# A decoder layer whose cross-attention keeps its SyncE transfers in program order, with the output steps of a batch one unit later

## The chip, the core and the metric

The kernel runs on one core of a Trainium2 chip. The core has a matrix engine (TensorE, "PE" in the profile, with its weight loads as "PEld"), three engines for elementwise work (VectorE "DVE", ScalarE "ACT", GpSimd "POOL") and SyncE ("SP"), which in this kernel issues most of the transfers. All transfers run on 16 DMA engines that the issuing engines share. The metric is the time of one execution on the device in microseconds; less is better.

## What is computed

One decoder layer in float32 over 16 batches of 128 tokens and 1024 channels. With `ln` for the layer norm:

```python
x = x + self_attn(ln(x))
x = x + cross_attn(ln(x), ctx, ctx)
x = x + ffn(ln(x))            # 4-bit weights, silu(gate) * up, down
```

The change touches only the cross-attention, which for each batch computes (8 heads of 64, the 128 tokens are the channels of its 1x1 convolutions, the 1024 model channels are its positions):

```python
qh = softmax(Wq @ q, over the 64 of a head) * 64**-0.5
kh = softmax(Wk @ k, over the positions)
context = kh @ vh.T                       # per head, 64 x 64
out = Wo @ (context.T @ qh) + bo
out = out / max(norm(out, over channels), 1e-12) * g * sqrt(128)
```

## The kernel before, in words

The program has three stages. In the first, self-attention runs and the first five blocks of the gate and up weights are unpacked beside it. The second is the cross-attention of batches 8 to 15 and then 0 to 7; in the profile it runs from about 250 us to about 850 us, the last part overlapping the third. The third is the feed-forward network, by nested matrix products with fewer multiplications, to the end.

**Units and ticks.** The cross-attention is cut into units, and after each unit `tick()` runs what is due. `later(n, fn)` puts `fn` off until the n-th tick from then; what falls due in one tick runs in the order in which it was put off. A batch has eight units, alternating: a key unit for the batch after it (`key_unit`, matmuls `kq<-wk_sb,cx`, then the exponential `ek` on ACT, and two ticks later the context matmuls `kx<-ek,cxt`) and a query unit for itself (`query_unit`, matmuls `kq<-wq_sb,xn`, then `qe` on ACT). The four query units of a batch are called `oc` 0 to 3.

**The way of a query unit.** `weigh` divides by the softmax sums: DVE reduces `qden`, POOL multiplies `qe` (132 us for all 64). `turn` then transposes 32 x 32 squares on DVE (`kt<-qe`) and stores the result to a buffer in DRAM (`kd<-kt`, line 817). One tick later `load` reads it back in another arrangement in four transfers (`qs<-kd`, line 822). `qs` has five buffers, each batch fills four. A later step consumes them: `project_out` has four `piece` steps of TensorE (`mm<-qs,m_sb`), one for each `qs`, then `norms` (`mm<-sq,ones`), then on DVE, one tick apart, a scaling of `y`, an addition to the residual `X`, the statistics of the next layer norm, its shift, and `turned`, which stores `X` to DRAM through POOL's queue and puts the normalised rows through a transpose (`kt<-xn`) and four more SP transfers (`xt<-kt`, line 579).

**When the outputs run.** The tuple `when` gives the ticks for the four pieces and `norms`, counted from the start of the batch, so a 12 is the fourth unit of the following batch:

```python
if len(ahead) == 2:
    when = (12, 13, 14, 15, 16, 1, 1)
elif ahead:
    when = (12, 13, 14, 15, 16, 1, 0)
else:
    when = (10, 10, 11, 11, 12, 1, 0)
```

**What sets the order of instructions.** A scheduler orders the instructions of every engine when the kernel is built. `InOrder` wraps an engine, so that each instruction given through it keeps its place in program order among the others given so. In this stage TensorE and VectorE are wrapped (`tensor`, `vector`; the profile shows their instructions under line 63). ScalarE, GpSimd and SyncE are not, so the scheduler may place a transfer of SyncE ahead of or behind others of the same queue. SyncE carries out its queue in order: a transfer that waits holds back all behind it.

**What lies around it.** At the start of the stage SP loads the weights of the cross-attention (`wk_sb`, `wq_sb`, the two halves of `wvo`, `xbo_sb`, `gs_sb`), the context of two batches in both arrangements (`cx`, `cxt`), and in `wo_again` the output weights of the self-attention, for the last four batches of which `give_half` still has to run (matmuls `mm<-wo_again,oT`, from the first tick on). At the end, SP loads the first weights of the feed-forward network (`w`, line 1081; the first pair through POOL's queue), and its matmuls (`p<-b,w`, line 1156) take the place of units, with a tick after each.

Of the kernel before, what the change touches and what calls it, by code (L numbers as in the profile page):

```python
# [18 lines left out]
P = 128  # L19
# [47 lines left out]
def decoder_layer(  # L67
# [28 lines left out]
    nc = tc.nc  # L96
# [435 lines left out]
    first.close()  # L532

    tensor, vector = InOrder(tc, nc.tensor), InOrder(tc, nc.vector)

# [33 lines left out]
    def turn_rows(b, xn, pool):  # L571

        kt = pool.tile([P, 4, 2 * JC, Q], F32, name="kt")
        vector.transpose(
            kt.rearrange("p c m t -> p m c t"), xn.rearrange("p m (c i) -> p m c i", c=4)
        )
        xt = xt_all[PASSES.index(b - b % HB)][b % HB]
        for a in range(4):
            nc.sync.dma_start(
                xt[a].rearrange("c i n j t -> i c (n j t)"),  # L580
                kt[ts(a, Q)].rearrange("i c m t -> i c (m t)"),
            )
# [36 lines left out]
    def later(n, fn):  # L619
        pend.append([n, fn])  # L620

    def tick():
        for p in pend:
            p[0] -= 1
        due = [p for p in pend if p[0] <= 0]
        for p in due:
            pend.remove(p)
        for p in due:
            p[1]()

    if True:
        wq_sb = bw.tile([P, HIDDEN], F32, name="wq_sb")
        wk_sb = bw.tile([P, HIDDEN], F32, name="wk_sb")
        wvo = b0.tile([P, 2, 4, S], F32, name="wvo", tag="xn2")
        wv_sb, xwo_sb = wvo[:, 0], wvo[:, 1]
        g_sb = bs.tile([P, HEADS, S], F32, name="g_sb")
        xbo_sb = bs.tile([P, 1], F32, name="xbo_sb")
        gs_sb = bs.tile([P, 1], F32, name="gs_sb")
        ones = bs.tile([P, P], F32, name="ones")
        nc.sync.dma_start(wk_sb, xwk)  # L640
        nc.sync.dma_start(wq_sb, xwq)
        nc.sync.dma_start(wv_sb, xwv.rearrange("(r p) s -> p r s", p=P))
        nc.sync.dma_start(xwo_sb, xwo.rearrange("(r p) o -> p r o", p=P))
        nc.sync.dma_start(xbo_sb, xbo)
        nc.sync.dma_start(gs_sb, xg)
        vector.tensor_scalar(gs_sb, gs_sb, math.sqrt(S), None, ALU.mult)
        vector.memset(ones, 1.0)
        if plain:
# [5 lines left out]
        def note(*both):  # L654
            if plain:
                for t, v in zip(totals, both):
                    t = t[:, : v.shape[1]]
                    nc.gpsimd.tensor_tensor(t, t, v, ALU.add)
# [14 lines left out]
        def mix_weights():  # L673

            D = DIM_HEAD
            for e in range(2):
                ps = bps.tile([P, 4, S], F32, name="mm")
                for r in range(4):
                    tensor.matmul(
                        ps[:, r, :],  # L680
                        wv_sb[ts(e, D), r, :],
                        xwo_sb[ts(e, D), r, :],
                        start=True,
                        stop=True,
                    )
                dst = g_sb.rearrange("p (r e) o -> p e r o", e=2)[:, e]
                nc.scalar.mul(dst, ps, D**-0.5)

        def load_ctx(b):
            c = bcx.tile([P, C], F32, name="cx")  # L690
            nc.sync.dma_start(c, cx[b])
            ct = bct.tile([P, NB, S], F32, name="cxt")
            nc.sync.dma_start(ct, cxt[b])
            return c, ct

        def key_shift(c_sb):
# [86 lines left out]
        def query_unit(xn, pair, qs, wait):  # L783

            wide = [P, 2 * HEADS, DIM_HEAD]
            ps = bpk.tile([P, 2, 512], F32, name="kq")
            for i in range(2):
                tensor.matmul(
                    ps[:, i, :], xn[:, ts(2 * pair + i, P)], wq_sb, start=True, stop=True
                )  # L790
            heads = ps.rearrange("p i (h d) -> p (i h) d", d=DIM_HEAD)
            qe = b3.tile(wide, F32, name="qe")
            if plain:
                nc.scalar.activation(qe, heads, AF.Exp)  # L794
            else:
                mx = small.tile([P, 2 * HEADS], F32, name="qmx")
                vector.tensor_reduce(mx, heads, AX.X, ALU.max)
                vector.tensor_tensor(qe, heads, mx.unsqueeze(2).to_broadcast(wide), ALU.subtract)
                nc.scalar.activation(qe, qe, AF.Exp)

            def weigh():
                den, rec = (small.tile([P, 2 * HEADS], F32, name=n) for n in ("qden", "qrec"))
                vector.tensor_reduce(den, qe, AX.X, ALU.add)
                vector.reciprocal(rec, den)
                nc.gpsimd.tensor_tensor(qe, qe, rec.unsqueeze(2).to_broadcast(wide), ALU.mult)  # L805
                note(den, rec)

            def turn():  # L810
                kt = bkt.tile([P, 4, NB, Q], F32, name="kt")
                vector.transpose(
                    kt.rearrange("p c n j -> p n c j"),
                    qe.rearrange("p h d -> p (h d)").rearrange("p (n c j) -> p n c j", c=4, j=Q),
                )
                kd = dram.tile([4, Q, 4, NB, Q], F32, name="kd", tag="kd", bufs=3)
                nc.sync.dma_start(kd.rearrange("a i c n j -> (a i) c n j"), kt)

                def load():
                    qt = qs[pair] = bqs.tile([P, 4, NB, Q], F32, name="qs", tag="qs")  # L820
                    for c in range(4):
                        nc.sync.dma_start(  # L822
                            qt[ts(c, Q)], kd[:, :, c].rearrange("a i n j -> i a n j")
                        )

                later(1, load)

            later(2, weigh)
            later(wait, turn)

        def turned(b):
# [65 lines left out]
        def rows(b):  # L897
            xn = b0.tile([P, C], F32, name="xn2", tag="xn2")
            row_shift(b, vector)
            normalise_act(xn, X[b], b)  # L900
            return xn
# [3 lines left out]
        def operand(q):  # L905

            b12 = blocks[0, 1]
            if q == 7:
                T0[7] = b12
                vector.tensor_tensor(b12, blocks[1, 1], b12, ALU.subtract)  # L910
                return
            t = T0[q] = xres.tile(
                [P, TOKENS, JC, Q], F32, name=f"T{q}", tag={5: "X0", 6: "X2", 4: "X4"}[q]
            )
            a, b = {
                5: (b12, blocks[0, 0]),
                6: (blocks[1, 1], T0.get(5)),
                4: (blocks[1, 0], T0.get(6)),
            }[q]
            vector.tensor_tensor(t, a, b, ALU.subtract)  # L920


        batches = [p + i for p in PASSES for i in range(HB)]
        ctxs = {b: load_ctx(b) for b in batches[:2]}
        wo_again = []
        for d in range(2):
            wo_again.append(bqs.tile([P, C], F32, name="wo_again", tag="qs"))
            nc.sync.dma_start(wo_again[d], wo[ts(d, P)])
        mix_weights()
        xns = {batches[0]: rows(batches[0])}  # L930

# [9 lines left out]
        for k, b in enumerate(batches):  # L941
            ahead = batches[k + 1 : k + 3]
            qs = {}


            if len(ahead) == 2:
                when = (12, 13, 14, 15, 16, 1, 1)
            elif ahead:
                when = (12, 13, 14, 15, 16, 1, 0)
            else:  # L950
                when = (10, 10, 11, 11, 12, 1, 0)
            project_out(b, qs, keys[b], when)
            if ahead:
                later(5, lambda n=ahead[0]: xns.update({n: rows(n)}))
            if len(ahead) == 2:
                later(2, lambda n=ahead[1]: ctxs.update({n: load_ctx(n)}))

            for n, q in {B - 3: [(5, 5)], B - 2: [(3, 7), (7, 6)], B - 1: [(6, 4)]}.get(k, ()):
                later(n, lambda q=q: operand(q))
            for oc in range(4):  # L960
                if ahead:
                    key_unit(ctxs[ahead[0]], oc, keys[ahead[0]])
                    tick()
                query_unit(xns[b], oc, qs, 4 if len(ahead) == 2 else 3)
                tick()
# [59 lines left out]
    with ExitStack() as gs:  # L1025

        def pool(name, bufs, **kw):
            return gs.enter_context(tc.tile_pool(name=name, bufs=bufs, reuse_waits="tile", **kw))

        cw = pool("c_w", 5)  # L1030
        ct = pool("c_t", 4)
# [868 lines left out]
```

## Time and profile before

| | |
|---|---|
| time, median of 3 runs | 2260.39 us (2260.33 to 2260.86) |
| time of the profiled execution | 2262.39 us |
| its span, first to last instruction | 2260.5 us |
| mean granted TensorE clock | 0.996 |
| TensorE matmuls busy | 2207.0 us, 98% of the span |
| VectorE busy | 1517.2 us, 67% |
| GpSimd busy | 555.6 us, 25% |
| ScalarE busy | 472.0 us, 21% |
| SP's transfers | 377.72 MB, 53.5% of the 16 DMA engines' time |

All times inside the execution are microseconds from the start of the span. "Busy" of TensorE counts pipelined matmuls. A wait is the idle time of an engine ahead of an instruction, with what ended it; a float32 matmul appears as two instructions, so four matmuls of a piece are "x8". "SPq" is SP's queue, and an entry there is the issue of a transfer, not its duration.

### The profile page before, as it was taken

What the parts mean: (1) busy time and instruction counts of PE and PEld (TensorE: products, weight loads), DVE (VectorE), ACT (ScalarE), POOL (GpSimd) and SP (SyncE); (2) the same over time, 40 slices, a digit from 0 to 9 for tenths busy, and PEclk for the clock granted to TensorE, in tenths of its full rate; (3) what the DMA queues carried; (4) which work ended last, traced back from release to release, by engine and by line L of the source; (5) the groups of instructions that cost most, each with busy time, mean ns of one, the idle gap of its engine ahead of it and who ended that gap; (6) DMA issues with size and microseconds to landing.
All of it is one profiled execution on the core that took longest, in us unless ns stands there. A gap on an engine that the chain in (4) does not pass through costs nothing.

```text
span 2260.5 us, 24112 instructions
## 1 busy us (share of the span) xinstructions
PE 2207.0 (98%) x8330; PEld 1517.4 (67%) x8330; DVE 1517.2 (67%) x2055; ACT 472.0 (21%) x651; POOL 555.6 (25%) x543
## 2 busy tenths in 40 slices
PE   8999999999998999999999999999999999999998
PEld 7556555555555554444774478888888688888887
DVE  6997467767777738756787668787787546544462
ACT  2111234544454441111111111122121000000000
POOL 5452044344444410000330034444442000000000
PEclk9999999999999999999999999999999999999999
DMA  6435256676696478888739843554554974433731
GB/s 249 156 130 185 75 149 182 199 197 178 196 277 175 149 207 288 282 269 268 220 131 288 278 126 126 191 179 151 191 182 160 354 225 147 133 123 128 224 117 39
DMA packets 270835, 425.23 MB, mean 188 GB/s; under 512 B 28784, under 2 KB 130544, under 8 KB 270576
## 3 DMA queue, kind: packets, MB, share of 16 engines
q1 hardware_dynamic: 244624, 377.72, 53.5%
q0 software_dynamic: 8064, 27.27, 3.3%
q10 hardware_dynamic: 18016, 18.62, 2.6%
q8 instruction: 68, 1.11, 0.2%
q14 instruction: 63, 0.52, 0.1%
HBM read 265.62 MB, written 157.35 MB: 187 GB/s over the span
## 4 chain that ended last, share of the span: by engine, by line
PE 86%; DVE 6%; DMA 3%; issue 3%; SPq 1%; ACT 1%; POOL 1%; DVEq 0%; POOLq 0%; ACTq 0%
PE po L1779 21%; PE q L63 20%; PE p L63 18%; PE kq L63 8%; PE mm L63 6%; PE kx L63 4%; PE mm L396 4%; DMA qs<-kd 2%; PE mm L411 2%; PE p L1156 1%; DVE pa L63 1%; PE mm L292 1%; SPq L822 1%; DVE kt L63 1%; PE tr L343 1%
## 5 line engine op out<-in xcount | busy, mean ns | idle before, releaser
L63 PE MATMUL p<-b,w 128*128 128x512 f32 x560 | 246.4, 592 | 0.0
L63 PE MATMUL q<-ti,li 128*128 128x256 f32 x1008 | 233.7, 381 | 3.5 <-DVE ti L63 2.8
L63 POOL TENSOR_TENSOR li<-w 128x512 f32<-128x512 f32 x84 | 118.3, 1410 | 430.7 <-DMA w<-wu 241.1
L63 PEld LDWEIGHTS q<-ti,li 128*128 128x128 f32 x1008 | 192.1, 191 | 31.6 <-issue 2.8
L63 PEld LDWEIGHTS p<-b,w 128*128 128x128 f32 x560 | 106.4, 190 | 133.1 <-issue 129.4
L1779 PE MATMUL po<-wc,lc 128*128 128x256 f32 x840 | 183.4, 379 | 0.0
L63 PE MATMUL p<-T,w 128*128 128x512 f32 x400 | 177.2, 592 | 0.0
L1779 PEld LDWEIGHTS po<-wc,lc 128*128 128x128 f32 x840 | 159.6, 190 | 21.7
L63 ACT COPY k<-q 128x512 f32<-128x512 f32 x126 | 73.7, 585 | 400.6 <-PE q L63 400.6
L63 PE MATMUL mm<-qs,m_sb 128*128 128x256 f32 x512 | 123.0, 384 | 21.2 <-DMA qs<-kd 21.2
L63 PEld LDWEIGHTS mm<-qs,m_sb 128*128 128x128 f32 x512 | 97.0, 191 | 64.7 <-issue 46.0
L63 PEld LDWEIGHTS p<-T,w 128*128 128x128 f32 x400 | 76.0, 190 | 95.7 <-issue 95.2
L805 POOL TENSOR_TENSOR qe<-qe,qrec 128x1024 f32<-128x1024 f32 x64 | 132.1, 2064 | 4.0 <-issue 0.2
L1779 PE MATMUL po<-wq,lq 128*128 128x256 f32 x560 | 126.7, 379 | 0.3 <-issue 0.3
L63 PE MATMUL kq<-wq_sb,xn 128*128 128x512 f32 x256 | 122.3, 602 | 0.0
L63 PE MATMUL kx<-ek,cxt 128*128 128x512 f32 x256 | 121.8, 598 | 0.0
L63 PE MATMUL kq<-wk_sb,cx 128*128 128x512 f32 x256 | 120.4, 592 | 0.0
L1779 PEld LDWEIGHTS po<-wq,lq 128*128 128x128 f32 x560 | 106.0, 190 | 15.9 <-issue 0.9
L63 DVE TENSOR_TENSOR pa<-pa,sz 128x1024 f32<-128x1024 int32 x86 | 113.8, 1324 | 2.5
L396 PE MATMUL mm<-xnT,wqkv_sb 128*128 128x512 f32 (+1 forms) x320 | 112.5, 507 | 0.0
L726 ACT ACTIVATE ek<-kq 128x1024 f32<-128x1024 f32 x64 | 65.5, 1023 | 182.1 <-PE kq L63 182.1
L63 DVE TENSOR_REDUCE qden<-qe 128x16 f32<-128x1024 f32 x64 | 76.4, 1194 | 29.6 <-ACT qe L794 29.6
(201 smaller groups left out, 3620.8 us busy)
## 6 DMA issues: line engine op xcount, KB each, us to landing
w<-wu SPq DMA_DIRECT2D x140, 256.0 KB, 3.6
lq<-h SPq DMA_DIRECT2D x140, 256.0 KB, 4.5
w<-wg SPq DMA_DIRECT2D x138, 256.0 KB, 2.8
kd<-kt SPq DMA_DIRECT2D x64, 512.0 KB, 3.0
qs<-kd SPq DMA_DIRECT2D x256, 128.0 KB, 4.1
h<-hc SPq DMA_DIRECT2D x80, 256.0 KB, 2.8
wq<-wd SPq DMA_DIRECT2D x70, 256.0 KB, 5.2
h<-h SPq DMA_DIRECT2D x60, 256.0 KB, 3.5
```

The lines of the kernel that those rows point to most:

```text
L63: return lambda *args, **kw: self._tc.keep_in_program_order(fn(*args, **kw))
L292: tensor.matmul(ps, oT[:, d, ts(b % BPT, S)], wo_d[d][:, ts(h, 512)], start=(d == 0), stop=(d == 1),)
L343: nc.tensor.transpose(tr[:, j, :], xn[:, ts(4 * h + j, P)], ident)
L396: nc.tensor.matmul(ps[:, tokens], wqkv_sb[:, f, c, :], xnT[:, c, tokens], start=(c == 0), stop=(c == CC - 1),)
L411: nc.tensor.matmul(ps, xnT[:, c, ts(i, S)], wqkv_sb[:, 4:6, c, :], start=(c == 0), stop=(c == CC - 1),)
L726: nc.scalar.activation(ek, ps, AF.Exp)
L805: nc.gpsimd.tensor_tensor(qe, qe, rec.unsqueeze(2).to_broadcast(wide), ALU.mult)
L822: nc.sync.dma_start(qt[ts(c, Q)], kd[:, :, c].rearrange("a i n j -> i a n j"))
L1156: tensor.matmul(ps, wt[:, j, :], T[q][:, :, j], start=(first == q and j == 0), stop=(q in (2, 3, 4) and j == JC - 1), skip_group_check=True,)
L1779: nc.tensor.matmul(bank[:, i, :], l[:, ts(i, S)], w,  start=(start and c == 0 and i % 2 == 0), stop=(stop and c == len(pairs) - 1), skip_g ...
```

## The change

A wrapper `sync = InOrder(tc, nc.sync)` is made beside those of TensorE and VectorE, and every transfer that the cross-attention issues on SyncE goes through it: the loads of weights and context at its start, `kd`, `qs`, `xt` and `wo_again`. The loads of the feed-forward network (`w`) and of the weight preparation stay outside. Besides, for a batch that has two more behind it, the four pieces and `norms` are due one tick later, and with `norms` all steps after it.

```diff
     tensor, vector = InOrder(tc, nc.tensor), InOrder(tc, nc.vector)
+    sync = InOrder(tc, nc.sync)
...
         for a in range(4):
-            nc.sync.dma_start(
+            sync.dma_start(
                 xt[a].rearrange("c i n j t -> i c (n j t)"),
...
-        nc.sync.dma_start(wk_sb, xwk)
-        nc.sync.dma_start(wq_sb, xwq)
-        nc.sync.dma_start(wv_sb, xwv.rearrange("(r p) s -> p r s", p=P))
-        nc.sync.dma_start(xwo_sb, xwo.rearrange("(r p) o -> p r o", p=P))
-        nc.sync.dma_start(xbo_sb, xbo)
-        nc.sync.dma_start(gs_sb, xg)
+        sync.dma_start(wk_sb, xwk)
+        sync.dma_start(wq_sb, xwq)
+        sync.dma_start(wv_sb, xwv.rearrange("(r p) s -> p r s", p=P))
+        sync.dma_start(xwo_sb, xwo.rearrange("(r p) o -> p r o", p=P))
+        sync.dma_start(xbo_sb, xbo)
+        sync.dma_start(gs_sb, xg)
...
             c = bcx.tile([P, C], F32, name="cx")
-            nc.sync.dma_start(c, cx[b])
+            sync.dma_start(c, cx[b])
             ct = bct.tile([P, NB, S], F32, name="cxt")
-            nc.sync.dma_start(ct, cxt[b])
+            sync.dma_start(ct, cxt[b])
...
                 kd = dram.tile([4, Q, 4, NB, Q], F32, name="kd", tag="kd", bufs=3)
-                nc.sync.dma_start(kd.rearrange("a i c n j -> (a i) c n j"), kt)
+                sync.dma_start(kd.rearrange("a i c n j -> (a i) c n j"), kt)
...
                     for c in range(4):
-                        nc.sync.dma_start(
+                        sync.dma_start(
                             qt[ts(c, Q)], kd[:, :, c].rearrange("a i n j -> i a n j")
                         )
...
             wo_again.append(bqs.tile([P, C], F32, name="wo_again", tag="qs"))
-            nc.sync.dma_start(wo_again[d], wo[ts(d, P)])
+            sync.dma_start(wo_again[d], wo[ts(d, P)])
...
             if len(ahead) == 2:
-                when = (12, 13, 14, 15, 16, 1, 1)
+                when = (13, 14, 15, 16, 17, 1, 1)
```

As built, the order of the instructions differs in these places. On SP, one batch in the steady part was `kd kd kd, qs qs, xt, qs, kd, cx, cxt, qs` (a `qs` stands for its four transfers) and is now `kd, qs, kd, qs, kd, xt, qs, kd, cx, cxt, qs`. At the start, SP's queue was `xbo_sb, gs_sb, cxt, cxt, wk_sb, wq_sb, wvo, wvo, cx, cx, wo_again, wo_again` and is now `wk_sb, wq_sb, wvo, wvo, xbo_sb, gs_sb, cx, cxt, cx, cxt, wo_again, wo_again`. On TensorE each piece and `norms` stand one unit later, so that `norms` now follows a key unit; the number of matmuls is the same. On VectorE `m_sb` now comes ahead of the scaling of `y`, and the statistics come after the next `qden`. At the end of the stage TensorE and SP have the same work in nearly the same order.

## The prediction

> **What bounds the kernel now.** I began with the page. TensorE is busy for 2207.0 of 2260.5 us and most of the chain that ended last is its work, so only TensorE's idle time and its clock can be gained. One group of the page has idle time in front of it on TensorE that this change can reach:
>
> ```profile
> PE 86%; DVE 6%; DMA 3%; issue 3%; SPq 1%; ACT 1%; POOL 1%; DVEq 0%; POOLq 0%; ACTq 0%
> L63 PE MATMUL mm<-qs,m_sb 128*128 128x256 f32 x512 | 123.0, 384 | 21.2 <-DMA qs<-kd 21.2
> ```
>
> Asked for the waits of TensorE from 293 to 765 us, the trace names nothing but these 21.2 us, in 10 waits: 1.5 to 2.1 us each and one of 4.3. So I laid one batch out in time: TensorE, SP's queue and the transposes of VectorE.
>
> ```profile
> 454.77 1.89 PE L63 MATMUL mm<-qs,m_sb 128*128 128x256 f32 x8
> 456.50 1.88 PE L63 MATMUL kx<-ek,cxt 128*128 128x512 f32 x4
> 458.22 1.88 PE L63 MATMUL kq<-wk_sb,cx 128*128 128x512 f32 x4
> 462.19 1.97 PE L63 MATMUL mm<-qs,m_sb 128*128 128x256 f32 x8 [2.10 <-DMA qs<-kd]
> ```
> ```profile
> 442.91 13.20 SPq L817 DMA_DIRECT2D kd<-kt  x3
> 456.20 4.12 SPq L822 DMA_DIRECT2D qs<-kd  x8
> 460.42 1.90 SPq L579 DMA_DIRECT2D xt<-kt  x4
> 462.57 2.03 SPq L822 DMA_DIRECT2D qs<-kd  x4
> ```
> ```profile
> 441.64 1.24 DVE L63 STREAM_TRANSPOSE kt<-qe 128x1024 f32<-128x1024 f32 x1
> 448.84 1.25 DVE L63 STREAM_TRANSPOSE kt<-qe 128x1024 f32<-128x1024 f32 x1
> 454.53 1.23 DVE L63 STREAM_TRANSPOSE kt<-qe 128x1024 f32<-128x1024 f32 x1
> ```
>
> The piece that waits is the fourth of the batch. By the ticks its operand (`oc` 3) is the transpose at 441.64, stored at 442.91. Its load, due a tick later, stands behind two further stores in SP's queue, and these wait for the transposes that end at 450.1 and 455.8. So it goes out at 456.2 instead of soon after 446, and TensorE, ready at 459.9 (458.22 and 1.72 of pace), starts at 462.19. The other pieces have over 10 us in hand. The list of SP's waits has this behind it: `kd` waits for the transpose 254.7 us in 48 times; a store early in the queue costs nothing, the load behind it does.
>
> **What the skill says.** The Trainium skill, DMA: Bandwidth & Descriptors, "Two DMAs through the same engine are not ordered", wants the issuing engine to wait for the first transfer's semaphore before a dependent one; the trace agrees (SP waits 14.7 us in all for `kd<-kt` ahead of `qs`), so every load costs SP the landing of its store. The same page, "Issuing engines are not separate DMA queues", has all transfers on the same 16 engines; at 248 to 256 us they are busy to 0.96 to 1.04, so added bytes there take time. TensorE: Matmul & The Clock Gate, "What's actually happening", puts the clock at half after an idle window of about 3.4 us; here also one wait of 2.1 us was followed by it, others of that length not. SBUF — State Buffer, "SBUF: two separate sides", has VectorE with two operands and GpSimd exclude each other; the trace agrees (a scaling of `y` takes 2.25 us beside GpSimd, 1.16 without).
>
> **The steady part.** What a batch costs without a wait: from the fourth piece at 331.26 to that at 395.61 lie two batches with one wait of 1.65 us, 64.35 us; from 428.60 to 462.19 one batch with one of 2.10, 33.59. The difference, 62.70 less 31.49, is 31.2 us without wait, and 0.25 us per wait beyond its idle time (restart). After two of the waits the clock is low:
>
> ```profile
> 596.00:600.00 4.00, 4.00 (x11) 2.55 (x12) 2.04 (x3) 1.26 (x2) 0.00 (x0) 0.64 1.04 279
> 600.00:604.00 4.00, 4.00 (x10) 1.85 (x9) 1.47 (x2) 2.43 (x4) 0.22 (x1) 0.93 0.81 279
> 729.00:733.00 4.00, 3.78 (x10) 2.78 (x11) 1.19 (x2) 1.01 (x2) 0.00 (x0) 0.66 1.06 275
> 785.00:789.00 4.00, 3.64 (x5) 1.68 (x6) 2.09 (x2) 1.44 (x2) 2.05 (x2) 0.59 1.02 273
> ```
>
> (The granted clock is the last but two.) That is 4 x 0.36 + 4 x 0.07 = 1.7 us each for the first two. In reach: 21.2 + 10 x 0.25 + 3.4 = 27.1 us.
>
> Does all of it go? In program order the load of `oc` 3 follows its own store: store at 442.9, landed about 3.0 us later (its row), four issues of 0.45: all out by 448, landed by 452. The piece is wanted at 459.9, and one unit later still (3.4 us). Each edit alone would cover the 2.25 us; I count 27.1 once. What is late next? SP: per batch 4 x (0.34 + 3.0 + 1.9) + 1.9 for `xt` + 0.7 for the contexts = 23.5 us of 31.2; behind a waiting load stands the next store, and behind that, with three `kt` buffers, a transpose. `qs` has five buffers: the load of the next batch's `oc` 1 is due at tick 16 and takes the buffer of the first piece, now at 13 instead of 12; three units are left. ScalarE: from `norms` to the mixing matmuls into its old PSUM bank there were two units (6.9 us) and is now one with the four small matmuls: about 4.3 us from the end of the first half, for an exponential (1.02) and a logarithm (0.6). VectorE: the shift now comes about 3 us later against TensorE; ScalarE's row normalisation (1.24) and the exponential (1.02) that the next `kx` needs queue behind it. Laying the durations end to end I find 1.1 to 2.5 us in hand there, the least anywhere. So nothing added: **-27.1**; if each of 13 batches lost 1 us there, -14.
>
> **The start.** The built order puts both `cxt` loads (2 x 512 KB), which went out at 221 us into idle DMA engines, behind `wk_sb`, which waits for the last self-attention matmul, and ahead of `wo_again`:
>
> ```profile
> 221.12 0.91 SPq L693 DMA_DIRECT2D cxt<-in_cxt  x2
> 245.80 0.33 SPq L640 DMA_DIRECT2D wk_sb<-in_xwk  x1
> 247.68 0.98 SPq L691 DMA_DIRECT2D cx<-in_cx  x2
> 248.76 0.84 SPq L928 DMA_DIRECT2D wo_again<-in_wo  x2
> ```
> ```profile
> 255.74 1.12 PE L63 MATMUL mm<-wo_again,oT 128*128 128x512 f32 x2 [0.19 <-DMA wo_again<-in_wo]
> 257.07 1.10 PE L63 MATMUL mm<-wo_again,oT 128*128 128x512 f32 x2 [0.21 <-DMA wo_again<-in_wo]
> ```
>
> TensorE already takes `wo_again` as it lands, so every added byte is on its path: 1.05 MB at the 369 to 393 GB/s of 252 to 256 us is 2.8 us, at the 291 GB/s of the whole burst (3.15 MB from 246.1 to 256.9) 3.6. I take **+2.8**, and for the clock after some 3 us of idle time **+1.5** (0 if it holds, 1.7 if not). The two more issues ahead (0.33 and 0.51) hide in this queue; `gs_sb` lands later, and VectorE meets it about where it does now (251.5). Bounds +2.8 and +5.3.
>
> **The end.** After 777.97 TensorE waits 5.5 us for the first `w`, which GpSimd issues at 782.28 behind a `qe` product that waits for VectorE, where `y`, a transpose and `X` precede `m_sb` and `qden`. Now `m_sb` and `qden` precede `y` and `X`, so the issue comes up to 3.3 us earlier; part is given back at the transpose chain that the first `p<-T,w` needs. I take **-1.5**, between -3.5 and +3 (the new order holds back a transfer). The feed-forward part has the same matmuls in the same order and goes to its end as before: 0, within 1.
>
> **The sum.** -27.1 + 2.8 + 1.5 - 1.5 = -24.3, on a span of 2260.5 us: 2236.2. The profiled execution took 2262.39, 1.9 more than its span and 2.0 more than the median of the runs, so the median should be 2260.4 - 24.3 = **2236 us**.
>
> **Rivals.** (a) The forecast, with the ends of its terms from -28.8 (start +2.8 and no clock loss, end -3.5, feed-forward -1) to -17.8 (start +5.3, end +3, feed-forward +1): 2231 to 2243, chance 0.75. (b) A new wait takes the place of the old: ScalarE's queue behind the later shift, 1 us in each of 13 batches, so 2236 + 13 = 2249. For it: the 1.1 us in hand. Against: VectorE has 6.5 us of idle time per batch to catch up. 0.14. (c) The other side: SP, now strictly serial, sets the pace. It does so when a store takes more than 4.9 us to land (7.7 us of slack over four stores); at 5.7 us a batch takes 3.2 us more, 13 batches 42, so 2278; level with before at about 5.4. For it: DMA engines at 1.0 in bursts, `b<-xt` at 6.0. Against: the median 3.0 of `kd`, and the bursts come from loads let out together, which the new order spreads. 0.05. (d) Start and end both at their best and more, below 2231: 0.03. (e) Nothing measurable, because the gain is eaten by start and waits: 0.03. That the change doesn't act at all is excluded by the built order.
>
> **How the numbers follow.** What this measurement can tell from no change is about 0.2%, 4.5 us. (a), (d) and nearly all of (b) are faster: 0.92; same 0.03; slower 0.05. For 8 in 10 the range takes (a) and, up to 2248, half of (b): 2231 to 2248.
>
> **What would show it.** Right: `qs<-kd` gone from TensorE's waits between 293 and 765 us; batches 31.2 us apart; SP's entries `kd` x1, `qs` x4 in turn; the first `wo_again` matmul near 258.5 with some 3 us of idle time before it and a low clock after; the last fourth piece some 23 us earlier. Wrong: waits of `kx` for `ek` or of `mm` for ScalarE (b); SP waiting for `kd<-kt` by tens of us and stores late (c); a longer wait for the first `w`. The forecast is most easily wrong in the start and the end, by 3 us each.

## The result and the profile after

The changed kernel took 2241.36 us (median of 4 runs, 2240.96 to 2242.18) against 2260.36 for the kernel before in the same measurement (4 runs, 2257.68 to 2260.86): a ratio of 0.9911, 95% interval 0.9898 to 0.9923. The profiled execution took 2241.3 us, its span 2239.5, its mean clock 0.996.

The page of the changed kernel, the chain that ended last and the group of the pieces:

```profile
PE 90%; DVE 6%; issue 2%; DMA 1%; POOL 1%; ACT 0%; SPq 0%; DVEq 0%; POOLq 0%; ACTq 0%
L63 PE MATMUL mm<-qs,m_sb 128*128 128x256 f32 x512 | 120.8, 379 | 0.0
```

The 21.2 us of idle time ahead of the pieces are gone, and TensorE's share of the chain rose from 86 to 90%. The batch that the prediction laid out in time, on TensorE (start, duration, what ran, the wait ahead of it in brackets), with the start of the stage ahead of it:

```profile
254.68 1.96 PE L63 MATMUL kq<-wk_sb,cx 128*128 128x512 f32 x4 [2.46 <-DMA cx<-in_cx]
259.69 3.67 PE L63 MATMUL mm<-wo_again,oT 128*128 128x512 f32 x4 [3.06 <-DMA wo_again<-in_wo]
...
429.60 1.89 PE L63 MATMUL mm<-qs,m_sb 128*128 128x256 f32 x8
...
460.83 1.89 PE L63 MATMUL mm<-qs,m_sb 128*128 128x256 f32 x8
```

The last two are the fourth pieces of two batches in a row: no wait, and 31.23 us apart. The first two are new waits at the start. SP's queue in the same batch, and the transposes that its stores wait for:

```profile
443.21 0.34 SPq L63 DMA_DIRECT2D kd<-kt  x1
445.86 2.14 SPq L63 DMA_DIRECT2D qs<-kd  x4
451.17 0.34 SPq L63 DMA_DIRECT2D kd<-kt  x1
453.81 1.73 SPq L63 DMA_DIRECT2D qs<-kd  x4
```
```profile
441.95 1.24 DVE L63 STREAM_TRANSPOSE kt<-qe 128x1024 f32<-128x1024 f32 x1
449.90 1.25 DVE L63 STREAM_TRANSPOSE kt<-qe 128x1024 f32<-128x1024 f32 x1
455.57 1.25 DVE L63 STREAM_TRANSPOSE kt<-qe 128x1024 f32<-128x1024 f32 x1 [1.96 <-POOL qe L806]
```

The load for the fourth piece is issued at 445.86, behind its own store alone, 15 us before the piece; before the change it went out at 456.2, 6.0 us before. What the DMA engines did at the start (window, length, busy time of five engines, granted clock, DMA share, GB/s):

```profile
249.00:250.00 1.00, 1.00 (x12) 1.00 (x11) 0.97 (x2) 0.45 (x1) 0.00 (x0) 1.00 0.77 158
250.00:251.00 1.00, 0.81 (x8) 0.65 (x7) 0.39 (x3) 0.73 (x3) 0.46 (x1) 1.00 0.76 66
260.00:264.00 4.00, 4.00 (x6) 1.54 (x6) 0.60 (x1) 0.00 (x0) 0.00 (x0) 0.61 0.02 6
```

Before, the same two microseconds moved 280 to 297 GB/s. The five engines are TensorE, its weight loads, VectorE, ScalarE and GpSimd. In the third window the clock is low, after 2.46 and 3.06 us of idle time.

To see where the time went I cut each trace at the same events: the last self-attention matmul group (`mm<-atT,v`), the first sum of keys (`mm<-ones,ksum`), the last piece ahead of the first feed-forward product, that product, the first product of the second feed-forward block, and the last matmul. The first column is the time to the first of these events, and the others up to "rest" are the stretches from each to the next. All are of one profiled execution each; the kernels below the second line are the experiments.

| kernel | to `atT,v` | start | steady | to first `w` product | block 0 | rest | span |
|---|---|---|---|---|---|---|---|
| before | 249.48 | 37.71 | 490.78 | 7.39 | 68.40 | 1399.06 | 2260.5 |
| changed | 248.41 | 43.97 | 463.55 | 6.78 | 67.56 | 1401.31 | 2239.5 |
| e1_order_only | 247.94 | 45.24 | 463.55 | 10.69 | 79.85 | 1397.53 | 2252.8 |
| e2_later_only | 247.96 | 38.35 | 503.16 | 7.01 | 66.74 | 1399.14 | 2270.6 |
| e12_pieces_later | 248.93 | 38.05 | 479.55 | 6.75 | 68.21 | 1399.36 | 2249.2 |
| e7_pairs_only | 248.75 | 38.46 | 528.64 | 6.99 | 66.97 | 1401.65 | 2299.4 |
| e11_ctx_too | 248.92 | 38.86 | 468.66 | 6.90 | 66.51 | 1401.41 | 2240.1 |
| e3_start_free | 248.83 | 37.55 | 463.55 | 6.98 | 67.54 | 1401.81 | 2235.0 |
| e4_tiny_last | 248.46 | 40.90 | 463.55 | 6.93 | 67.40 | 1401.39 | 2237.3 |
| e13_tiny_scalar | 248.94 | 41.34 | 463.55 | 7.06 | 67.73 | 1401.52 | 2238.8 |
| e14_cxt_last | 248.30 | 38.77 | 463.55 | 6.90 | 66.52 | 1401.47 | 2234.0 |
| e5_last_later | 247.92 | 44.64 | 463.75 | 9.37 | 77.94 | 1404.00 | 2256.1 |
| e6_last_early | 248.80 | 41.11 | 463.55 | 8.10 | 73.81 | 1397.75 | 2241.4 |
| e10_both_ends | 247.95 | 38.28 | 463.75 | 1.73 | 65.92 | 1399.70 | 2225.8 |

From before to changed: -1.07 in the first stage, +6.26 at the start, -27.23 in the steady part, -0.61 and -0.84 at the end of the stage, +2.25 in the rest and +0.24 behind the last matmul: -21.0, the difference of the spans. The first column varies between 247.9 and 249.5 over all these traces, so its -1.07 is scatter. By the medians only 19.0 us were gained, since the profiled execution of before (2262.39) lay 2.0 above the median of its runs and that of the changed kernel did not.

### The profile page after: what moved, and what is told of

It reads as the page before. It is cut to its first block, busy times and chain, and to the rows that moved or that the text cites. A ratio compares the mean times of both kernels' runs of the same rounds, so it can differ in the third digit from the quotient of the medians.

```text
span 2239.5 us, 24114 instructions
## 1 busy us (share of the span) xinstructions
PE 2204.4 (98%) x8330; PEld 1517.3 (68%) x8330; DVE 1482.2 (66%) x2055; ACT 468.9 (21%) x651; POOL 553.1 (25%) x543
## 4 chain that ended last, share of the span: by engine, by line
PE 90%; DVE 6%; issue 2%; DMA 1%; POOL 1%; ACT 0%; SPq 0%; DVEq 0%; POOLq 0%; ACTq 0%
PE po L1780 21%; PE q L63 20%; PE p L63 18%; PE kq L63 9%; PE mm L63 8%; PE kx L63 5%; PE mm L396 4%; PE mm L411 2%; DVE pa L63 2%; PE p L1157 1%; PE mm L292 1%; PE tr L343 1%; DVE ti L63 1%; DMA wo_again<-in_wo 0%; POOL qe L806 0%
## 5 line engine op out<-in xcount | busy, mean ns | idle before, releaser
L806 POOL TENSOR_TENSOR qe<-qe,qrec 128x1024 f32<-128x1024 f32 x64 | 122.0, 1906 | 11.5 <-DVE qrec L63 9.3
L63 DVE STREAM_TRANSPOSE kt<-qe 128x1024 f32<-128x1024 f32 x64 | 79.5, 1242 | 43.7 <-POOL qe L806 43.5
```

The lines of the kernel that those rows point to most:

```text
L63: return lambda *args, **kw: self._tc.keep_in_program_order(fn(*args, **kw))
```

## The experiments

The experiments ran on three chips on which the kernel before takes 2265 to 2268 us (2262.6 to 2272.3 in single runs) instead of 2260. Whether one of them beats the kernel before is read from its ratio on the same chip. The changed kernel was not run on these chips, so the ratios can't be set against its 0.9911 (e6 below has the better ratio and the longer time). Nor was the kernel before traced there: the first line of the table may be some us too short to compare with, wherever that kernel waits. The kernels that have lost these waits agree to 0.2 us in the steady part on all chips, and among them I compare the stretches. First the two edits apart.

### e1_order_only: the order without the later due times

```diff
-                when = (13, 14, 15, 16, 17, 1, 1)
+                when = (12, 13, 14, 15, 16, 1, 1)
```

> Program order on SyncE, outputs at their old ticks. My theory (the fourth piece waits because its load stands behind two stores in SyncE's queue): the load goes out some 10 us earlier, so TensorE's 21.2 us of waits for qs between 293 and 765 us are gone, and the steady part costs as little as with both edits; the start loses its 6 us as there. About 2241, within 2 of the changed kernel. Rival (the later unit does the work, the order only tidies): the waits stay at 1 to 2 us per batch, above 2255.

Measured: 2256.19 us, ratio 0.996 (0.9946 to 0.9974), span 2252.8. The time is 15 us above what I expected, but the steady part is as expected: 463.55 us, to the hundredth that of the full change, without one wait for `qs`. What is lost is at the end, where TensorE has these waits:

```profile
PE mm L63 <- DVE within L63: 10.1, 1, 10.1
PE p L1157 <- DMA w<-wg: 8.8, 1, 8.8
```

So the order alone cures the steady part, and costs 3.9 us more than the full change ahead of the first feed-forward product and 12.3 in block 0. In the built order TensorE's last pieces stand later among the products of block 0 (the last piece at 824.33, the last `norms` at 827.78, against 806.81 and 810.25 in the changed kernel), and `within` (a check on the sums of the softmax, behind the last batch's statistics on VectorE) is late.

### e2_later_only: the later due times without the order

```diff
-                when = (12, 13, 14, 15, 16, 1, 1)
+                when = (13, 14, 15, 16, 17, 1, 1)
```

applied to the kernel before.

> Outputs one unit later, SyncE left to the scheduler (its queue as built: three stores, then two loads, as before; start of the stage as before). My theory: TensorE wants the fourth piece 3.4 us later, which covers the 2.25 us of lateness but not the one wait of 4.3: at most some 3 us of waits for qs left, and no loss at the start. About 2235 to 2238, less than the changed kernel. Rival (only the order cures it, the lateness moves along with the unit): waits of 1 to 2 us per batch stay, above 2250.

Measured: 2271.35 us, ratio 1.0018 (1.0010 to 1.0026): a little slower than before, as the rival had it. TensorE waits for `qs` 27.1 us in 13 waits, one in every batch, instead of the 21.2 in 10 of the first chip, and the steady part is 503.16 us. TensorE and SP of one batch:

```profile
465.83 1.97 PE L63 MATMUL mm<-qs,m_sb 128*128 128x256 f32 x8 [1.88 <-DMA qs<-kd]
```
```profile
446.18 13.96 SPq L817 DMA_DIRECT2D kd<-kt  x3
460.23 4.10 SPq L822 DMA_DIRECT2D qs<-kd  x8
```

The load stands behind the two further stores as before. The sum of keys of this batch is at 441.15, and the three transposes start 3.8, 11.7 and 17.4 us after it; before they started 2.6, 9.8 and 15.5 us after theirs (439.01). The piece is wanted 1.7 us later (its wait begins 22.8 us after the sum instead of 21.1), and the transpose at which the queue is let go comes 1.9 us later. The third transpose waits for GpSimd's product:

```profile
458.54 1.25 DVE L63 STREAM_TRANSPOSE kt<-qe 128x1024 f32<-128x1024 f32 x1 [1.96 <-POOL qe L805]
```

The divisors of this product are formed on VectorE behind the second transpose, and the second transpose stands behind the scaling of `y`, the addition to `X`, the statistics and the shift, which the same edit had moved.

### e12_pieces_later: the pieces later, the steps after them not

That reading can be tried: due times of the four pieces one later, `norms` and all that follows where they were, on the kernel before.

```diff
-                when = (12, 13, 14, 15, 16, 1, 1)
+                when = (13, 14, 15, 16, 16, 1, 1)
```

> SyncE as before; the four pieces due one unit later, norms and all steps after it at their old places, so that VectorE's scaling of y, X and the statistics come no later. Theory of why the later due times alone did not help: a unit is only 1.7 us there, and moving norms pushed the transposes of the next batch 1.1 to 2.0 us back on VectorE, which the loads wait for. Then here the transposes stand where they stood before (the third 15.5 us after the sum of keys, not 17.4), the fourth piece needs its load at 22.6 us after that sum and gets it at about 23.2: waits for qs of about 0.5 us each, under 8 us in all, against 27.1. Instead TensorE waits for ScalarE's square ahead of norms, about 1.5 us in each of 14 batches. Rival (the load comes as much later as the piece, whatever VectorE does): qs is waited for about 2 us in most batches again.

Measured: 2251.84 us, ratio 0.9938 (0.9916 to 0.9961). The waits of TensorE from 293 to 765 us:

```profile
PE mm L63 <- ACT sq L868: 7.0, 14, 0.5
PE mm L63 <- DMA qs<-kd: 3.3, 5, 1.9
```

The third transpose starts 15.5 us after the sum of keys (452.18 after 436.68) as it did before, and the waits for `qs` fall from 27.1 to 3.3 us. The square that `norms` needs costs 0.5 us a batch by the trace, a third of what I had put. So the later due times do help, if VectorE's share of them stays behind.

### e7_pairs_only and e11_ctx_too: which entries of the queue must be held

Both have the later due times. In the first only `kd` and `qs` go through `sync`, in the second also the contexts (all but the first two):

```diff
+    sync = InOrder(tc, nc.sync)
...
-                nc.sync.dma_start(kd.rearrange("a i c n j -> (a i) c n j"), kt)
+                sync.dma_start(kd.rearrange("a i c n j -> (a i) c n j"), kt)
...
-                        nc.sync.dma_start(
+                        sync.dma_start(
                             qt[ts(c, Q)], kd[:, :, c].rearrange("a i n j -> i a n j")
                         )
```

> Later due times, and the order of the program for the stores kd and the loads qs alone; weights, contexts and transfers of rows stay with the builder. Theory (the gain comes from the pairs alone, everything else in the order only costs, at the start): the steady part at 463.6 us without a wait for qs, the start as before (about 37.6 us from the last self-attention matmul to the first sum of keys), the built order after it as with the start free, so the wait for sg stays: span about 2235, time about 2235. Rival (the places of xt or of the contexts in the order also matter): some waits for qs come back, over 2238.

Measured: 2305.02 us, ratio 1.0178 (1.0159 to 1.0198), slower than before, with waits for `qs` of 46.1 us in 12. My theory fell, and the list of SP's own waits has the reason:

```profile
SPq L692 <- PE kq L63: 146.6, 12, 13.9
```
```profile
460.06 0.34 SPq L63 DMA_DIRECT2D kd<-kt  x1
474.42 0.35 SPq L692 DMA_DIRECT2D cx<-in_cx  x1
474.83 1.85 SPq L63 DMA_DIRECT2D qs<-kd  x4
```

The scheduler, free to place the context's load `cx`, set it ahead of a `qs` load, at a point where its buffer was still being read; there it waits 12 us on average, 14 in the case shown, and holds the pair behind it.

> The pairs kd and qs and the contexts' loads in the order of the program, later due times; xt and the first loads stay with the builder. New theory after the run with the pairs alone (there the builder set each cx load ahead of a qs load, where it waited 12 us for its buffer, 146.6 us in 12 waits, and held the pairs behind it): with the contexts held as well the steady part is 463.6 us again and no wait for qs is left, span about 2235. Rival (the two halves of xt that the builder now sets between pairs do it too, as each waits for its transpose): the steady part stays above 480 and qs is waited for, span over 2250.

Measured: 2241.76 us, ratio 0.9889 (0.9872 to 0.9905). The steady part is 468.66 us, with one wait for `qs` left (3.0 us). With the contexts held, 60 of e7's 65 us of excess over 463.55 are gone. The other 5.1 are this one wait and a stretch of low clock behind it (3.4 us at 0.50). In this kernel the scheduler cuts `xt` in two halves between the pairs, and they wait 86.6 us on SP's queue for their transposes; whether that makes the one `qs` late was not tested.

### e3_start_free, e4_tiny_last, e13_tiny_scalar, e14_cxt_last: the start

All four have both edits. In e3 the loads at the start (weights, the two small ones, two contexts, `wo_again`) go through `nc.sync` again, as before. In e4 the two small loads and the scaling of `gs_sb` stand behind `wo_again` in the order, in e13 they are issued by ScalarE, and in e14 they stay and the first two `cxt` go behind `wo_again`:

```diff
-        sync.dma_start(xbo_sb, xbo)
-        sync.dma_start(gs_sb, xg)
+        nc.scalar.dma_start(xbo_sb, xbo)
+        nc.scalar.dma_start(gs_sb, xg)
```
```diff
             ct = bct.tile([P, NB, S], F32, name="cxt")
-            sync.dma_start(ct, cxt[b])
+            if first:
+                put_off.append(lambda: sync.dma_start(ct, cxt[b]))
...
             sync.dma_start(wo_again[d], wo[ts(d, P)])
+        for load in put_off:
+            load()
```

> Both edits, but the loads at the start of the stage (weights, first two contexts, wo_again) outside the program order again, so that SyncE has them as in the kernel before; kd, qs, xt and the later contexts stay in order. My theory (the changed kernel loses 6.3 us at the start through this order: 2.5 for cx, 3.1 for wo_again, 1.6 for the clock, less 0.9 that was there): 2235. Rival (the loss is not of the order but of something else in that stretch): 2241 as the changed kernel.

> Both edits, all in program order, but xbo_sb and gs_sb (one float to a partition) after wo_again instead of ahead of cx. My theory (the two small transfers let the DMA engines move only 66 to 158 GB/s at 249 to 251 us and so hold cx back): the wait of 2.5 us for cx is gone, that for wo_again stays within 1 us, 2239. Rival (the small loads cost nothing, only the 1 MB of cxt does): the sum of both waits stays 5.5 us, 2241.

> The full change, but the two loads of one float per partition (xbo_sb, gs_sb) issued by ScalarE, off SyncE's order; the contexts stay ahead of wo_again. The start (from the last self-attention matmul to the first sum of keys) took 37.7 us before, 41.1 to 45.2 in the four kernels with the whole start in order (44.0 in the changed one), 40.9 in the one run with the two loads behind wo_again. Theory (the two small loads, where they stand ahead of cx, hold the large ones back by some 3 us): 40.5 to 41.5 us again and no wait for cx. Rival (40.9 was scatter; the small loads cost nothing): 43 to 45, with a wait for cx.

> The full change with the small loads where they are, but the two cxt loads (1.05 MB) moved behind wo_again in the order. Theory (3.2 us of the start are these bytes ahead of wo_again, 3.1 the small loads): the start is 40.5 to 41.5 us, a wait for cx of about 2 stays, wo_again is no longer waited for by more than 1. Rival (the loads all come late because the queue is let go only when the last self-attention matmul has ended, whatever their order): 43 to 45.

Measured: e3 2234.48 us, ratio 0.9863 (0.9848 to 0.9879), its start 37.55 us, as before the change. So the whole of the start's loss comes from the order of these loads. e4: 2239.84, ratio 0.9889 (0.9874 to 0.9904); e13: 2240.36, ratio 0.9883 (0.9863 to 0.9903); their starts are 40.90 and 41.34 us, and neither waits for `cx`. e14: 2236.51, ratio 0.9873 (0.9850 to 0.9896), its start 38.77 us, with these waits:

```profile
253.11 1.96 PE L63 MATMUL kq<-wk_sb,cx 128*128 128x512 f32 x4 [1.22 <-DMA cx<-in_cx]
255.58 1.12 PE L63 MATMUL mm<-wo_again,oT 128*128 128x512 f32 x2 [0.52 <-DMA wo_again<-in_wo]
```

From the start of `mm<-atT,v` to the first `wo_again` matmul it is 11.3 us in the changed kernel, 8.4 and 8.5 in e4 and e13, and 7.3 in e14. Before, it is 6.3, but the six experiments whose start is built as before (e2, e3, e7, e10, e11 and e12) have 6.1 to 7.4, so about 1 us is scatter here. So the contexts' bytes ahead of `wo_again` cost 1.0 to 2.4 us without the small loads (e4 and e13 against these seven), and 4.0 with them (the changed kernel against e14). With all its loads in order the start is the least steady stretch: e1, e5, e6 and the changed kernel took 45.2, 44.6, 41.1 and 44.0 us in all and 11.3, 10.6, 9.7 and 11.3 to the first `wo_again` matmul. So the two small loads cost 1.1 to 2.9 us more where the contexts follow (these four against e4 and e13), and where they don't (e14) nothing that stands out from the scatter. I had expected the two costs to add up, and they don't: e14's start is below the 40.5 us that I had put, and e4 still waits 2.7 us for `wo_again`.

How they cost it shows in SP's queue, of the changed kernel and of e4 (`wk_sb` goes out at 244.73 and 244.78):

```profile
246.93 0.34 SPq L63 DMA_DIRECT2D xbo_sb<-in_xbo  x1
247.80 0.42 SPq L63 DMA_DIRECT2D cx<-in_cx  x1
249.84 1.43 SPq L63 DMA_DIRECT2D wo_again<-in_wo  x2
```
```profile
246.65 0.50 SPq L63 DMA_DIRECT2D cx<-in_cx  x1
248.89 0.94 SPq L63 DMA_DIRECT2D wo_again<-in_wo  x2
```

Behind their entries `cx` goes out 1.2 us and `wo_again` 1.0 us later. That is nearly the whole cost in e6, and it is there in e14 too. The rest, up to 1.9 us, is slower landing: the first `wo_again` lands 8.2 us (e6) to 9.8 us (changed, e1) after its issue, against 7.9 and 8.0 in e4 and e13. The rates at 249 to 251 us fit this only loosely: 158 and 66 GB/s in the changed kernel, 250 and 172 in e6, 354 and 419 in e4, but 92 and 242 in e14, where `wo_again` lands in 6.8 us.

The low clock adds 1.0 to 1.4 us in the changed kernel, e4 and e13, and 2.5 to 2.6 in e1 and e5: from the first `wo_again` matmul to the sum of keys they take 32.5 to 32.8 and 34.0 to 34.1 us, against 31.5 where the clock holds (before, e6, e14).

### e5_last_later and e6_last_early: where the later due times matter

With the order kept, is it the due times of the last batch before the end that save e1's 16 us? In e5 only the last of the fourteen batches that have two more behind them has the later ones, in e6 all but that one.

```diff
-                when = (13, 14, 15, 16, 17, 1, 1)
+                when = (13, 14, 15, 16, 17, 1, 1) if k == len(batches) - 3 else (12, 13, 14, 15, 16, 1, 1)
```

(e5; in e6 the two tuples are exchanged.)

> Both the order and the due times, but the later due times only in the last of the fourteen batches that have two more behind them; the thirteen before it keep 12, 13, 14, 15, 16. The order alone cost 10.7 us from the last piece before the feed-forward part to its first matmul and 79.9 us from there to the second half of its first block, where the full change has 6.8 and 67.6. Theory A (the place at which the builder lets the last pieces in between the first feed-forward products follows from all the batches before; in the built order of this kernel they stand as late as with the order alone): 10 and 80 us again, span about 2252. Rival B (the due times of the last such batch alone decide it): 7 and 68 us, span about 2240. The steady part stays at 463.6 us in both.

> The reverse: the order, later due times in the thirteen batches and the old ones in the last of the fourteen. Theory A: 7 us to the first feed-forward matmul and 68 to the second half of its block, and, since the raw weights of the next block stand ahead of the last transfer of rows in SyncE's order as they did before, no wait of TensorE for sg: 2.5 us less after that, span about 2237. Rival B: 10 and 80 us, span about 2252.

Measured: e5 2257.94 us, ratio 0.9963 (0.9947 to 0.9978); e6 2243.17, ratio 0.9896 (0.9876 to 0.9916). e5 has 9.4 and 77.9 us at the end, nearly e1's; e6 has 8.1 and 73.8, a third and a half of the way from the changed kernel to e1. So neither alone does it: of the 16.2 us between e1 and the changed kernel, the last batch alone recovers 3.2 (e5) and the thirteen earlier ones 8.6 (e6). Their due times shift the place at which the scheduler lets the last pieces in between the first feed-forward products, whose matmuls it orders itself. Why it places them so is not settled by these runs.

### e10_both_ends: the two waits that the change leaves at the end

On top of e3, the first weights of the feed-forward network are issued by ScalarE instead of GpSimd, and the last batch's `xt` by GpSimd instead of SyncE.

```diff
-            load_weights(nc.gpsimd if n == 0 else nc.sync)
+            load_weights(nc.scalar if n == 0 else nc.sync)
...
+        queue = nc.gpsimd if b == PASSES[-1] + HB - 1 else sync
         for a in range(4):
-            sync.dma_start(
+            queue.dma_start(
                 xt[a].rearrange("c i n j t -> i c (n j t)"),
```

> As the kernel with the start freed (span 2235.0), with two transfers moved off SyncE and GpSimd: the first tile of feed-forward weights is issued by ScalarE, and the last transfer of rows (xt) by GpSimd. Theory: the wait for the first w shrinks from 5.1 us to about 2 (ScalarE reaches it behind a softmax exponential near 750, GpSimd reached it at 753.7), the clock after it keeps up better (1 us), and with the raw weights no longer behind the last xt on SyncE the wait for sg (2.2 us) and what follows it (3.8 us in all) go: span about 2227. Rival 1 (the weights' landing is bound by the DMA engines or by the tile's release, not by the issue): the wait for w stays at 5, span 2231. Rival 2 (sg is late for VectorE's own work, not for the raw weights): its wait stays at 2, span 2231.

Measured: 2226.52 us, ratio 0.9821 (0.9805 to 0.9837), the fastest kernel of the study. ScalarE's queue and the first product:

```profile
748.47 0.82 ACTq L1083 DMA_DIRECT2D w<-wg  x2
```
```profile
751.71 3.60 PE L1158 MATMUL p<-b,w 128*128 128x512 f32 x8
```

The weights go out 5.2 us earlier than in e3 (753.7 there), land in 2.9 us, and the product follows the last piece (749.98) without a wait and without the slow clock that came after it (0.50 at 757 to 761 us in e3): 5.3 us less to the first product, 1.6 less in block 0. The wait for `sg` is gone, and the rest is 2.1 us shorter than in e3.

## Why the prediction was right, and where it was not

The forecast of 2236 us, range 2231 to 2248, against 2241.36: the direction and the mechanism were right and the time lies in the forecast's own range (2231 to 2243), but 5.3 us of the gain were missing. By the steps of the prediction:

**The steady part, -27.1: right.** It measured -27.23. The terms can be told apart: the waits were 21.2 us, the clock fell to 0.50 twice for 3.41 us before and not at all after, which is 3.4 us, and the 2.6 that remain are 0.26 for each of ten restarts (the prediction's own differences gave 0.28, and it took 0.25). Seven traces with the steady part in order agree at 463.55 us (two more have 463.75), so nothing was added: no new wait of `kx` or of the mixing matmuls (rival b), and SP waited 122.9 us for `kd<-kt` in 48 waits, 2.6 us each, below the 3.0 that I had put and far from the 4.9 of rival (c).

**"Each edit alone would cover the 2.25 us": wrong for the second edit.** The order does it alone (e1). The later due times alone gave nothing (e2, ratio 1.0018). The step that failed is "one unit later still (3.4 us)": the unit here is a query unit, and the piece moved by 1.7 us; and I counted the move for the piece, not for VectorE's steps that move with it and stand ahead of the transposes. I had seen that the shift comes later and asked only whether ScalarE would suffer. e12, which leaves these steps in place, shows it.

**The start, +4.3: measured +6.26.** That is above my upper bound of 5.3, but it is the difference of two single executions. The seven traces with the old order took 37.6 to 38.9 us here and the four with the new one 41.1 to 45.2, which is 5.6 between their means. The term for the bytes (2.8) lies between the 1.0 to 2.4 and the 4.0 that the experiments show, and the clock's (1.5) is close to its 1.2 in the changed kernel. What failed is "The two more issues ahead (0.33 and 0.51) hide in this queue". They don't hide: they put `wo_again`, for which TensorE was waiting already, 1.0 us further back, and in the changed kernel it then took 1.9 us longer to land than in e4. I had put nothing for this; it measured 1.1 to 2.9 us. The Trainium skill, DMA: Bandwidth & Descriptors, "Specifications", puts the least transfer for line rate at 512 bytes, and these move 4 bytes a partition; that they can delay large ones behind them it does not say there. The runs show it where the contexts follow, and e14 shows that it need not be.

**The end, -1.5: right in the sum** (-0.61 and -0.84), and in part by luck. I had the first `w` going out up to 3.3 us earlier. It goes out 3.8 us after the last piece (759.70) instead of 4.3, and the wait for it falls from 5.5 to 4.9 us. The first product then takes longer, as the clock stays low for longer (6.3 us to the next piece instead of 5.0), and the wait for `within`, which I had not counted, falls from 2.4 to 0.6. And e1 shows that I had no grip on it: the same two stretches cost 16.2 us more than in the changed kernel with an edit that I would have priced at nothing.

**The feed-forward part, "0, within 1": wrong, +2.25.** I argued that it "has the same matmuls in the same order", and looked at TensorE alone. Between the two traces TensorE has a new wait there:

```profile
852.94 12.26 PE L63 MATMUL p<-b,w 128*128 128x512 f32 x24 [1.91 <-DVE sg L63]
```

SP's queue of before and of the changed kernel, where the raw weights of a later block and the last batch's rows meet:

```profile
838.19 0.56 SPq L197 DMA_DIRECT2D raw<-in_gq  x1
...
846.70 1.78 SPq L579 DMA_DIRECT2D xt<-kt  x4
```
```profile
822.35 1.77 SPq L63 DMA_DIRECT2D xt<-kt  x4
824.16 0.56 SPq L197 DMA_DIRECT2D raw<-in_gq  x1
```

Before, the raw weights were ahead of `xt`; now they are behind it, and `xt` waits for the last transpose. VectorE's unpacking waits for them:

```profile
828.53 0.76 DVE L63 TENSOR_SCALAR pa<-raw 128x512 int32<-128x512 int32 x2 [3.56 <-DMA raw<-in_gq]
```

`sg` (851.61) then comes late on VectorE, behind more of this unpacking. My list of changes in the built order did not have this exchange. Over all fourteen traces the rest takes 1397.5 to 1399.7 us where `raw` is ahead of the last `xt` or `xt` is on another queue (before, e1, e2, e6, e12, e10), and 1401.3 to 1404.0 where it is behind; the wait for `sg` stands in each of these eight and in none of the six others. e10 moves `xt` away and the wait is gone; it also starts block 0 earlier, and no run moves this one transfer alone. But with fourteen traces divided in this way I take it as shown.

**The sum.** -24.3 was forecast for the span and -21.0 measured: +2.0 from the start and +2.3 from the rest, less 1.1 of scatter in the first stage. The other 2.0 us of the miss lie in the profiled execution of before: I saw that it was 2.0 above the median and took the difference of spans off the median all the same. The waits that I counted may be part of what put that execution above its median, and then the saving should have been cut by as much; the other executions have no trace to show it.

## What to carry to other kernels

Where a queue is carried out in order, a load that depends on a store costs what stands between the two; look for it in the queue's own list, not in the waiting engine's. But holding some entries of a queue in order lets a scheduler move the others to worse places (e7: 146.6 us of waits for one free load in each batch), and holding all of them drags along what was well placed, such as early loads into idle DMA engines; hold the steady part and leave the start free (e3). When work is put off by a unit, write down everything that moves with it and what on each engine then stands behind it, and follow the order of every queue into the next stage, not only that of the engine that bounds.

## What I had not expected of the hardware

Two transfers of 512 bytes, one float in each of 128 partitions, ahead of large ones cost 1.1 to 2.9 us where 2 MB stood between them and the load that TensorE waited for (the changed kernel, e1, e5 and e6 against e4 and e13): 1.0 us in the issuing queue, and up to 1.9 us in the landing of that load. With 1 MB between (e14) they cost nothing beyond the scatter.

The clock fell after idle times of 2.1 to 3.1 us at the start in the changed kernel, e1, e4, e5 and e13 (down to 0.50), but stayed at 1.00 after 3.08 us in e6. The length of the wait does not decide it; where the wait lies does. In every trace the changes of the clock that come between 245 and 900 us lie on a grid of 3.41 us. The fourteen traces have 2623 such stretches at full clock. All 40 in which TensorE was busy for less than 1.4 us were followed by a stretch at 0.50, none of the 2568 with 1.6 us or more, and 3 of the 15 between. The changed kernel and e6, each cut at its grid (TensorE's busy time comes third, the clock last but two):

```profile
256.28:259.70 3.42, 0.37 (x2) 0.01 (x1) 0.00 (x0) 1.02 (x1) 0.00 (x0) 1.00 0.80 323
259.70:263.11 3.41, 3.41 (x4) 1.46 (x5) 0.00 (x0) 0.00 (x0) 0.00 (x0) 0.50 0.03 10
```
```profile
253.88:257.29 3.41, 1.49 (x4) 0.38 (x2) 0.00 (x0) 2.04 (x4) 0.00 (x0) 1.00 1.02 419
257.29:260.70 3.41, 2.03 (x4) 0.79 (x5) 0.00 (x0) 0.00 (x0) 0.00 (x0) 1.00 0.40 162
260.70:264.12 3.42, 3.42 (x9) 1.52 (x8) 0.69 (x1) 1.02 (x1) 0.00 (x0) 1.00 0.02 5
```

The wait of e6 lies across two stretches and leaves enough work in each. A low stretch costs up to 3.41 x 0.5 = 1.7 us.

The steady part, once nothing waits, is the same to 0.01 us in seven executions on at least three chips, where the kernel before varied by up to 9 us in whole from run to run on one.
